# Turning normalised tokens with VectorE's 32x32 transpose and DMAs through DRAM instead of TensorE

## The chip, the cores and the metric

The kernel runs on one core of a Trainium2 chip. TensorE (PE) multiplies, VectorE (DVE) and ScalarE (ACT) work on elements, GpSimd (POOL) does a few odd operations, and SyncE (SP) issues nearly all DMAs. The metric is the device time of one execution in microseconds. Before the change it is 1166.89 us, the median of 3 runs (1166.68 to 1167.87).

## What is computed

The reference is a transformer of two layers on x of shape (4, 512, 256), all in fp32. Each of the four steps normalises its input first and adds its result to x:

```python
x = x + _L0_attn_ref(_layernorm(x, axis=-1), L0_attn_w_project, L0_attn_w_out)
x = x + _L0_ffn_ref(_layernorm(x, axis=-1), L0_ffn_router_w, L0_ffn_router_b, L0_ffn_expert_w, L0_ffn_expert_b)
x = x + _L1_attn_ref(_layernorm(x, axis=-1), L1_attn_w_qkv, L1_attn_w_proj)
x = x + _L1_ffn_ref(_layernorm(x, axis=-1), L1_ffn_gate_W_packed, L1_ffn_gate_scales, L1_ffn_up_W_packed, L1_ffn_up_scales, L1_ffn_down_W_packed, L1_ffn_down_scales)
```

Layer 0's attention is causal, with 16 heads of 16, over 512 tokens. Its second step mixes 8 experts: for each of 256 outputs the two best of 8 router logits weigh the experts' products, so there are two dense products of 256 x 2048 for every token. Layer 1's attention has 16 heads of 128 in 4 groups, and it reads the axis of length 4 as the sequence: each token attends to 4 tokens. Its last step is a gated unit of 2048 inner units (tanh GELU of a gate times an up product, then a down product) whose weights come as 4-bit codes with scales.

## The kernel before

**Layout.** The 2048 tokens lie in `xres` as 16 tiles of 128 tokens with 256 features each. Four tiles form a block (`NBLK` = 4), so a normalised block `xn` is 128 x 4 x 256. The host has put the tokens in such an order that, in each tile, every 32 partitions hold a closed set of layer 1's short sequences.

**Turning.** Products need the features on the partitions: `xT` is 128 x 2 x 512 (two halves of the features, 512 tokens). `transposed` (line 206) turns one half of a block with four TensorE transposes of 128 x 128 against an identity into one PSUM tile of the pool `dn` (two buffers, shared with most products), and ScalarE copies it to SBUF. There are sixteen such conversions: four for layer 0's attention (`inputs_T`, line 571), which the change leaves alone, and the twelve that it touches, whose PSUM tiles are named `xT_ps`: the four blocks of the experts (`hidden_pieces`, line 264), the four of layer 1's attention (`start_pieces` with `into_T`, lines 989 and 981), and the four of the gated unit (`first_pieces`, line 1122, makes the first one, `x_first`; `normed_T`, line 213, the other three). In the experts' blocks the copy of the second half adds 16 to the last feature (`last_16`, line 86), with which the biases are folded into the weights.

**Order.** Until the gated unit, PE, DVE, POOL and ACT run in the order in which the code is written (`manual_schedule`, line 73); SP does so only through the first batches (line 899), and after that the framework's scheduler orders it, where earlier code has precedence. The written order comes from a planner: work beside the attention is cut into pieces by generators, each `yield need(engine, cost, gap, cond)` says what a piece costs (about microseconds), how many slots must have passed since the stream's last piece and on what condition it may go; `fill` (line 149) is one slot and emits ready pieces, stream by stream, until the slot's budgets of PE and DVE are used up. Streams inserted at the front go first. The paces of the experts' pieces follow `made()`, the number of finished steps of the weights.

**Stages.** Layer 0's attention fills the first 385 us or so, with the projections and the experts' pieces between its batches. Block b of the experts starts when block b of the attention is done (line 811). `logit_pieces` and `result_pieces` call `dense` (line 230), whose stationary operand is 128 columns of `xT`. Then layer 1's pools open, `wqkv` is loaded by ten DMAs and `wpj` by one (lines 963 to 973), and `start_pieces(0)` goes first in the slots (line 1148); it issues the turning, then four pieces of values (line 1001). For each of 16 pairs of block and group, `project1`, `score`, `softmax_1`, `softmax_2`, `mix` and `output` follow, with slots between them. `start_pieces(j + 1)` starts while the first group of block j is worked on. When the experts are done, the 4-bit weights are loaded and decoded in further pieces (`weight_in_pieces`, line 1128) and `x_first` is made. In the gated unit (lines 1214 to 1281) all engines are ordered by the framework's scheduler. `inner(j)` makes gate and up products for 16 groups of 128 inner units (`gate_up`, line 946) and the tanh GELU; `down(j)` follows one block later.

Of the kernel before, what the change touches and what calls it, by code (L numbers as in the profile page):

```python
# [8 lines left out]
F32 = mybir.dt.float32  # L9
# [7 lines left out]
P = 128  # L17
# [15 lines left out]
def tile_transformer(  # L33
# [48 lines left out]
    nc.vector.memset(half_t, 0.5)  # L82
    minus_12 = const.tile([P, 1], F32, name="minus_12")
    nc.vector.memset(minus_12, -12.0)

    last_16 = const.tile([P, 1], F32, name="last_16")
    nc.vector.tensor_scalar(last_16, ident[:, P - 1 : P], 16.0, None, ALU.mult)

    mask32 = const.tile([P, 32], F32, name="mask32")
    nc.vector.tensor_reduce(  # L90
# [23 lines left out]
    def need(engine, cost, gap=0, cond=None):  # L114
        return engine, cost, gap, cond
# [83 lines left out]
    def layernorm(j, pool, small, deinterleave=False):  # L199
# [3 lines left out]
        normed.clear()  # L203
        return out[0]

    def transposed(xn, hc, ps_pool, tag, name):

        ps = ps_pool.tile([P, 4, P], F32, tag=tag, name=name)
        for t in range(4):
            nc.tensor.transpose(ps[:, t, :], xn[:, t, hc * P : (hc + 1) * P], ident)  # L210
        return ps

    def normed_T(j, pool, small, ps_pool, tag, deinterleave=False, out_pool=None):
        xn = layernorm(j, pool, small, deinterleave)
        xT = (out_pool or pool).tile([P, 2, 512], F32, tag="xT", name=f"xT{j}")
        for hc in range(2):
            ps = transposed(xn, hc, ps_pool, tag, f"xT_ps{j}_{hc}")
            nc.scalar.copy(xT[:, hc, :], ps.rearrange("p t q -> p (t q)"))
        return xT

    def add_residual(g, ps):
        nc.vector.tensor_tensor(xres[:, g, :], xres[:, g, :], ps, ALU.add)  # L222
# [7 lines left out]
    def dense(ps, g, w, pair):  # L230

        xT = xTs[g // 4]
        for hc in range(2):
            nc.tensor.matmul(  # L234
                ps, lhsT=xT[:, hc, (g % 4) * P : (g % 4 + 1) * P],
                rhs=w[:, hc, 2 * pair : 2 * pair + 2, :].rearrange("p e o -> p (e o)"),
                start=hc == 0, stop=hc == 1,
            )
# [25 lines left out]
    def hidden_pieces(b):  # L264

        out = []
        done = (4 * b - 5, 1)
        last = b == NBLK - 1
        yield from norm_pieces(b, b1, b2, out, cond=lambda: b < 2 or done in halves)
        xT = b2.tile([P, 2, 512], F32, tag="xT", name=f"xT{b}")  # L270
        for hc in range(2):
            yield need("PE", 0.5, 0 if hc else 1 + last)
            ps = transposed(out[0], hc, ps_dn, "dn", f"xT_ps{b}_{hc}")
            ps = ps.rearrange("p t q -> p (t q)")
            if hc:
                nc.scalar.activation(xT[:, hc, :], ps, AF.Identity, bias=last_16)
            else:
                nc.scalar.copy(xT[:, hc, :], ps)
        normed.clear()
        xTs[b] = xT  # L280

    def logit_pieces():
# [663 lines left out]
    def gate_up(ps, w, xT, jj, par):  # L946
        for half in range(2):
            nc.tensor.matmul(  # L948
                ps, lhsT=wgu[:, w, half, jj, par * P : (par + 1) * P], rhs=xT[:, half, :],
                start=half == 0, stop=half == 1,  # L950
            )

# [6 lines left out]
    with ExitStack() as l1:  # L959
# [20 lines left out]

        def into_T(out, to, name):

            for hc in range(2):
                yield need("PE", 0.5, 0 if hc else 2)
                ps = transposed(out[0], hc, ps_dn, "dn", f"{name}_ps{hc}")
                nc.scalar.copy(to[:, hc, :], ps.rearrange("p t q -> p (t q)"))  # L986
            normed.clear()

        def start_pieces(j):

# [34 lines left out]
        def score(p):  # L1025

            qT, kT = state.pop("qk")
            ps = ps_dn.tile([P, 4, HPK, 32], F32, tag="dn", name=f"s1_{p}")
            for t in range(4):
                for c in range(NC):  # L1030
                    at = t * P + 32 * c
                    nc.tensor.matmul(  # L1032
                        ps[32 * c : 32 * c + 32, t], lhsT=kT[:, at : at + 32],
                        rhs=qT[:, :, at : at + 32], start=True, stop=True,
                    )
            state["s"] = ps
# [44 lines left out]
        def mix(p):  # L1081
            j, kv = divmod(p, NKV)
            v, pT = state[j][1], state.pop("p")
            avs = [
                ps_a.tile([P, 4, HPK, 32], F32, tag="a", name=f"a_{p}_{c}") for c in range(NC)
            ]
            for t in range(4):
                for c in range(NC):
# [125 lines left out]
    with ExitStack() as f1:  # L1214
        wd_p = f1.enter_context(tc.tile_pool(name="f1_w", bufs=1))
        d2 = f1.enter_context(tc.tile_pool(name="f1_2", bufs=2))
        d1 = f1.enter_context(tc.tile_pool(name="f1_1", bufs=1))
        d3 = f1.enter_context(tc.tile_pool(name="f1_3", bufs=3))
        ps_gu = f1.enter_context(tc.tile_pool(name="f1_gu", bufs=2, space=PSUM))
        ps_o = f1.enter_context(tc.tile_pool(name="f1_o", bufs=2, space=PSUM))  # L1220

        wd = wd_p.tile([P, NJ, 2, HID], F32, name="wd")

        def inner(j):
            xT = normed_T(j, d2, d2, ps_dn, "dn", deinterleave=True) if j else x_first
            it = d2.tile([P, NJ, 2, 512], F32, tag="it", name=f"it{j}")
            for jj in range(NJ):
                for par in range(2):
                    n = f"{j}_{jj}_{par}"
                    if firsts:  # L1230
                        gp, up = firsts
                        firsts.clear()
                    else:
                        gp = ps_gu.tile([P, 512], F32, tag="g", name=f"g_{n}")
                        up = ps_gu.tile([P, 512], F32, tag="u", name=f"u_{n}")
                        gate_up(gp, 0, xT, jj, par)
                        gate_up(up, 1, xT, jj, par)
# [5 lines left out]
                    nc.vector.tensor_tensor(sq, sq, gp, ALU.mult)  # L1243
                    nc.scalar.activation(th, sq, AF.Tanh, scale=0.7978845608028654)  # L1244
                    nc.vector.scalar_tensor_tensor(th, th, 1.0, gp, ALU.add, ALU.mult)  # L1245
                    nc.vector.scalar_tensor_tensor(
                        it[:, jj, par, :], th, 0.5, up, ALU.mult, ALU.mult
                    )
                if j < 2 and jj % 4 == 3:
                    at = 4 * j + 2 * (jj // 4)  # L1250
                    for _ in dequant_pieces(
                        d2, d1, f"d{at}", [down_w[at + i] for i in range(2)],
                        [
                            lambda b, i=i: down_s[at + i, b : b + 1, :].to_broadcast([16, HID])
                            for i in range(2)
                        ],
                        wd[:, at : at + 2], lambda emit, slots=1: emit(),
                    ):
                        pass
            return it  # L1260

        def down(j, it):
            for t in range(4):
                ps = ps_o.tile([P, HID], F32, tag="o", name=f"y_{j}_{t}")
                for c in range(2 * NJ):
                    nc.tensor.matmul(  # L1266
                        ps, lhsT=it[:, c // 2, c % 2, t * P : (t + 1) * P],
                        rhs=wd[:, c // 2, c % 2, :], start=c == 0, stop=c == 2 * NJ - 1,
                    )
                add_residual(4 * j + t, ps)  # L1270
# [4 lines left out]
        pending = None  # L1275
        for j in range(NBLK):
# [62 lines left out]
```

## Time and profile before

| what | us |
|---|---|
| median of 3 runs | 1166.89 |
| span of the profiled execution | 1164.9 |
| PE busy | 1144.1 |
| DVE busy | 812.4 |
| ACT busy | 481.9 |
| transposes on `xT_ps` (96) and their weight loads, PE busy | 15.6 and 11.5 |

The profiled execution's own time beside its span is not recorded; its span is 2.0 us below the runs' median. In the profile, busy time counts instructions between their start and end, and matmuls overlap in the pipeline, so a busy PE is not PE at its peak: the distance between two starts is the better measure. An idle time in brackets ends with what released the instruction. "issue" stands for waits that the profile does not show. A timeline row merges instructions of one kind; its second column is then the stretch from the first start to the last end.

### The profile page before, as it was taken

Reading aid. Unit: us, or ns where it says so; the run is one execution under the profiler, and the core shown is the slowest. Engines: PE = TensorE matmul, PEld = TensorE weight load, DVE = VectorE, ACT = ScalarE, POOL = GpSimd, SP = SyncE. Lnnn points to the kernel's source line nnn. Section 1 sums busy time; section 2 is a strip of 40 time slices with the busy share of each in tenths; the row PEclk is TensorE's granted clock in tenths of the full one; section 3 lists DMA queues with packets and bytes.
Section 4 is the critical chain, followed back from the end, with each engine's and each line's share of the span. In section 5 each row is a group of like instructions: output and inputs, shape, how many; then the busy total and the mean of one; then the engine's idle time right before and its main releaser. Section 6 shows DMA issues by size and latency. Waiting matters only on the chain.

```text
span 1164.9 us, 18575 instructions
## 1 busy us (share of the span) xinstructions
PE 1144.1 (98%) x7182; PEld 662.6 (57%) x7182; DVE 812.4 (70%) x1788; ACT 481.9 (41%) x1095; POOL 108.2 (9%) x153
## 2 busy tenths in 40 slices
PE   9999999999998999999999999999999999999998
PEld 5666555555554445555555555566544475484487
DVE  6675899999988844868663776687699835716710
ACT  1444555555655542444443444444344313303300
POOL 8322221212112000000000000000000000000000
PEclk9999999999999999999999999999999999999999
DMA  4440100000000500000000001110110000000000
GB/s 130 118 120 2 27 12 1 2 2 2 2 2 1 181 1 1 1 1 0 1 1 1 1 1 46 33 51 19 27 46 1 0 1 19 0 1 19 1 19 18
DMA packets 21527, 26.46 MB, mean 23 GB/s; under 512 B 5160, under 2 KB 15144, under 8 KB 21440
## 3 DMA queue, kind: packets, MB, share of 16 engines
q1 hardware_dynamic: 20624, 24.10, 7.6%
q10 hardware_dynamic: 816, 1.18, 0.4%
q8 instruction: 56, 0.92, 0.3%
q14 instruction: 31, 0.25, 0.1%
HBM read 18.97 MB, written 2.10 MB: 18 GB/s over the span
## 4 chain that ended last, share of the span: by engine, by line
PE 82%; DVE 13%; issue 2%; ACT 1%; POOL 1%; SPq 0%; DMA 0%; POOLq 0%; DVEq 0%; ACTq 0%
PE qk_ps L1019 11%; PE y L1266 9%; PE o L1110 9%; PE g L948 9%; PE u L948 9%; PE lg_ps L234 8%; PE eo L234 7%; PE s L668 3%; PE s L716 3%; DVE mx L687 3%; PE av L752 2%; PE v_ps L1001 2%; PE qk_ps L539 2%; PE a L1090 1%; PE s L1032 1%
## 5 line engine op out<-in xcount | busy, mean ns | idle before, releaser
L1019 PE MATMUL qk_ps<-xT,wqkv 128*128 128x512 f32 x320 | 148.9, 599 | 2.3 <-ACT part L323 1.2
L234 PE MATMUL lg_ps<-rw,xT 128*128 128x512 f32 x256 | 122.5, 601 | 1.4 <-ACT xT L986 0.3
L234 PE MATMUL eo<-ew,xT 128*128 128x512 f32 x256 | 121.5, 600 | 0.8 <-ACT lg L297 0.5
L1110 PE MATMUL o<-wpj,oT 128*128 128x256 f32 x512 | 119.1, 382 | 0.0
L1266 PE MATMUL y<-wd,it 128*128 128x256 f32 x512 | 111.8, 379 | 0.0
L1110 PEld LDWEIGHTS o<-wpj,oT 128*128 128x128 f32 x512 | 95.9, 190 | 27.5 <-issue 14.3
L1266 PEld LDWEIGHTS y<-wd,it 128*128 128x128 f32 x512 | 97.0, 190 | 15.0 <-issue 2.2
L687 DVE TENSOR_REDUCE mx<-s 128x1 f32<-128x384 f32 (+3 forms) x176 | 100.5, 633 | 0.2 <-PE s L681 0.2
L1019 PEld LDWEIGHTS qk_ps<-xT,wqkv 128*128 128x128 f32 x320 | 59.1, 190 | 71.4 <-issue 57.4
L725 ACT ACTIVATE pt<-s 128x512 f32<-128x512 f32 (+1 forms) x176 | 84.1, 565 | 35.9 <-PE s L716 35.9
L948 PE MATMUL g<-xT,wgu 128*128 128x512 f32 x192 | 90.4, 593 | 0.0
L948 PE MATMUL u<-xT,wgu 128*128 128x512 f32 x192 | 90.2, 592 | 0.0
L323 ACT ACTIVATE part<-eo,c 128x256 f32<-128x256 f32 x128 | 53.6, 471 | 84.7 <-PE eo L234 74.8
L735 POOL TENSOR_SCALAR_AFFINE_SELECT pt<-pt 128x256 f32<-128x256 f32 (+2 forms) x88 | 62.4, 716 | 246.9 <-ACT pt L725 246.7
L1244 ACT ACTIVATE th<-sq 128x512 f32<-128x512 f32 x64 | 40.3, 630 | 87.8 <-DVE sq L1243 87.8
L234 PEld LDWEIGHTS lg_ps<-rw,xT 128*128 128x128 f32 x256 | 46.1, 190 | 46.1 <-issue 37.3
L234 PEld LDWEIGHTS eo<-ew,xT 128*128 128x128 f32 x256 | 46.1, 190 | 45.7 <-issue 38.3
L222 DVE TENSOR_TENSOR xres<-xres,y 128x256 f32<-128x256 f32 x16 | 6.7, 421 | 92.5 <-PE y L1266 92.5
L297 ACT COPY lg<-lg_ps 128x512 f32<-128x512 f32 x64 | 37.6, 588 | 73.5 <-PE lg_ps L234 73.5
L185 POOL TENSOR_TENSOR ln_rs<-rs_v,minus_half 128x4 f32<-128x4 f32 x15 | 16.6, 1103 | 552.2 <-DVE rs_v L184 440.0
L1245 DVE SCALAR_TENSOR_TENSOR th<-th,g 128x512 f32<-128x512 f32 x63 | 43.2, 686 | 29.3 <-ACT th L1244 29.2
L948 PEld LDWEIGHTS u<-xT,wgu 128*128 128x128 f32 x192 | 36.5, 190 | 45.9 <-issue 44.7
(240 smaller groups left out, 1782.5 us busy)
## 6 DMA issues: line engine op xcount, KB each, us to landing
qk<-stage SPq DMA_DIRECT2D x56, 64.0 KB, 2.4
wqkv<-in_w_qkv SPq DMA_DIRECT2D x8, 320.0 KB, 6.4
rw<-in_router_w SPq DMA_DIRECT2D x8, 256.0 KB, 4.8
ew<-in_expert_w SPq DMA_DIRECT2D x8, 256.0 KB, 5.5
wpj<-in_w_proj SPq DMA_DIRECT2D x1, 2048.0 KB, 12.5
out<-xres SPq DMA_DIRECT2D x4, 512.0 KB, 2.7
xres<-in_x SPq DMA_DIRECT2D x3, 512.0 KB, 4.8
dq_wgu<-in_gate_w SPq DMA_DIRECT2D x8, 128.0 KB, 2.4
```

The source lines that it names most:

```text
L234: nc.tensor.matmul(ps, lhsT=xT[:, hc, (g % 4) * P : (g % 4 + 1) * P], rhs=w[:, hc, 2 * pair : 2 * pair + 2, :].rearrange("p e o -> p (e o) ...
L297: nc.scalar.copy(lg[:, 2 * pair : 2 * pair + 2, :].rearrange("p e o -> p (e o)"), ps)
L323: nc.scalar.mul(part[:, e % 4], ps[:, i], c[:, e : e + 1])
L687: nc.vector.tensor_reduce(maxes[n % 2][:, h, gs[0] : gs[0] + nb], ps[:, : nb * nk].rearrange("p (b k) -> p b k", b=nb), AX.X, ALU.max,)
L725: nc.scalar.activation(pt[:, i, : nb * nk], tiles[2 * pair + i][:, : nb * nk], AF.Exp, scale=0.25)
L735: nc.gpsimd.affine_select(out=last, in_=last, compare_op=ALU.is_ge, fill=0.0, base=0, pattern=pattern, channel_multiplier=-1,)
L948: nc.tensor.matmul(ps, lhsT=wgu[:, w, half, jj, par * P : (par + 1) * P], rhs=xT[:, half, :], start=half == 0, stop=half == 1,)
L1019: nc.tensor.matmul(ps, lhsT=wqkv[:, hc, kv, h, :], rhs=xT[:, hc, :], start=hc == 0, stop=hc == 1,)
L1110: nc.tensor.matmul(ys[t // 2][:, t % 2], lhsT=state["o"][:, h, t * P : (t + 1) * P], rhs=wpj[:, HPK * kv + h, :], start=kv == 0 and h == 0 ...
L1244: nc.scalar.activation(th, sq, AF.Tanh, scale=0.7978845608028654)
L1245: nc.vector.scalar_tensor_tensor(th, th, 1.0, gp, ALU.add, ALU.mult)
L1266: nc.tensor.matmul(ps, lhsT=it[:, c // 2, c % 2, t * P : (t + 1) * P], rhs=wd[:, c // 2, c % 2, :], start=c == 0, stop=c == 2 * NJ - 1,)
```

## The change

Tokens of the twelve conversions are turned in another way. VectorE transposes each 32 x 32 square of `xn` in one instruction, which leaves each group of 32 partitions with its own tokens but the features of all 8 groups of 32 along the row. Four DMAs, one for each 32 partitions, write these rows to a DRAM tile `by_hidden`, sorted by feature (runs of 512 B), and a fifth reads them back over `xT` with the features on the partitions (runs of 2 KB). All five are issued on SP. The columns of `xT` are then in another order: 32 tokens of tile 0, of tile 1, and so on for each group of 32 partitions. For the experts the transpose writes with a step of four, so that a tile is every fourth column, and `dense` reads every fourth column. Layer 1's attention, where a token needs only its own 32 partitions, takes columns and partitions in the new order; `gate_up` reads the columns in runs of 32 in the old one. The addition of 16 is a VectorE instruction on one column of `xn`. In the plan a conversion is one DVE piece, and the stream may go on three slots later. In the gated unit, norm and turning of the next block are written in the third of the eight steps of `inner`. The 96 transposes and 24 ScalarE copies go.

```diff
-    last_16 = const.tile([P, 1], F32, name="last_16")
-    nc.vector.tensor_scalar(last_16, ident[:, P - 1 : P], 16.0, None, ALU.mult)
...
+    rows_out = ctx.enter_context(
+        tc.tile_pool(name="rows_out", bufs=2, space=bass.MemoryType.DRAM)
+    )
+
+    def turned(xn, xT, name, tiles_inside=False):
+
+        order = "p h (b j t) -> p (h b) t j" if tiles_inside else "p h (b t j) -> p (h b) t j"
+        nc.vector.transpose(
+            xT.rearrange(order, t=4, j=32), xn.rearrange("p t (b j) -> p b t j", j=32)
+        )
+        by_hidden = rows_out.tile([HID, 4, P], F32, tag="by_hidden", name=f"{name}_rows")
+        for a in range(4):
+            nc.sync.dma_start(
+                out=by_hidden.rearrange("(b i) a x -> a i b x", i=32)[a],
+                in_=xT[32 * a : 32 * a + 32].rearrange("p h (b x) -> p (h b) x", x=P),
+            )
+        nc.sync.dma_start(out=xT, in_=by_hidden.rearrange("(h p) a x -> p h (a x)", p=P))
...
-    def normed_T(j, pool, small, ps_pool, tag, deinterleave=False, out_pool=None):
...
     def dense(ps, g, w, pair):
...
-                ps, lhsT=xT[:, hc, (g % 4) * P : (g % 4 + 1) * P],
+                ps, lhsT=xT[:, hc, g % 4 :: 4],
...
     def hidden_pieces(b):
...
-        for hc in range(2):
-            yield need("PE", 0.5, 0 if hc else 1 + last)
-            ps = transposed(out[0], hc, ps_dn, "dn", f"xT_ps{b}_{hc}")
-            ps = ps.rearrange("p t q -> p (t q)")
-            if hc:
-                nc.scalar.activation(xT[:, hc, :], ps, AF.Identity, bias=last_16)
-            else:
-                nc.scalar.copy(xT[:, hc, :], ps)
+        yield need("DVE", 1.5)
+        nc.vector.tensor_scalar(
+            out[0][:, :, HID - 1], out[0][:, :, HID - 1], 16.0, None, ALU.add
+        )
+        turned(out[0], xT, f"xT{b}", tiles_inside=True)
         normed.clear()
+        yield need("PE", 0.0, 3)
         xTs[b] = xT
...
     def gate_up(ps, w, xT, jj, par):
         for half in range(2):
             nc.tensor.matmul(
-                ps, lhsT=wgu[:, w, half, jj, par * P : (par + 1) * P], rhs=xT[:, half, :],
+                ps.rearrange("p (t a j) -> p t a j", a=4, j=32),
+                lhsT=wgu[:, w, half, jj, par * P : (par + 1) * P],
+                rhs=xT[:, half].rearrange("p (a t j) -> p t a j", t=4, j=32),
...
         def into_T(out, to, name):
 
-            for hc in range(2):
-                yield need("PE", 0.5, 0 if hc else 2)
-                ps = transposed(out[0], hc, ps_dn, "dn", f"{name}_ps{hc}")
-                nc.scalar.copy(to[:, hc, :], ps.rearrange("p t q -> p (t q)"))
+            yield need("DVE", 1.4)
+            turned(out[0], to, name)
             normed.clear()
+            yield need("PE", 0.0, 3)
...
         def score(p):
...
-                    at = t * P + 32 * c
+                    at = c * P + 32 * t
                     nc.tensor.matmul(
-                        ps[32 * c : 32 * c + 32, t], lhsT=kT[:, at : at + 32],
+                        ps[32 * t : 32 * t + 32, c], lhsT=kT[:, at : at + 32],
...
         def mix(p):
...
-                    r = slice(32 * c, 32 * c + 32)
+                    r = slice(32 * t, 32 * t + 32)
                     nc.tensor.matmul(
-                        avs[c][:, t], lhsT=v[r, t, kv, :], rhs=pT[r, t], start=True, stop=True
+                        avs[t][:, c], lhsT=v[r, c, kv, :], rhs=pT[r, c], start=True, stop=True
                     )
-            oq = oT.rearrange("p h (t c q) -> p c t h q", c=NC, q=32)
+            oq = oT.rearrange("p h (t c q) -> p t c h q", c=NC, q=32)
...
         def inner(j):
-            xT = normed_T(j, d2, d2, ps_dn, "dn", deinterleave=True) if j else x_first
+            xT = xTs.pop(j)
...
+                if jj == 2 and j + 1 < NBLK:
+                    xTs[j + 1] = d2.tile([P, 2, 512], F32, tag="xT", name=f"xT2_{j + 1}")
+                    turned(
+                        layernorm(j + 1, d2, d2, deinterleave=True), xTs[j + 1], f"xT2_{j + 1}"
+                    )
```

More of the change, by code (lines that the diff above doesn't have):

```diff
@@ L211, in transposed @@
         return ps
-    def normed_T(j, pool, small, ps_pool, tag, deinterleave=False, out_pool=None):
-        xn = layernorm(j, pool, small, deinterleave)
-        xT = (out_pool or pool).tile([P, 2, 512], F32, tag="xT", name=f"xT{j}")
-        for hc in range(2):
-            ps = transposed(xn, hc, ps_pool, tag, f"xT_ps{j}_{hc}")
-            nc.scalar.copy(xT[:, hc, :], ps.rearrange("p t q -> p (t q)"))
-        return xT
     def add_residual(g, ps):
@@ L267, in hidden_pieces @@
         done = (4 * b - 5, 1)
-        last = b == NBLK - 1
         yield from norm_pieces(b, b1, b2, out, cond=lambda: b < 2 or done in halves)
         xT = b2.tile([P, 2, 512], F32, tag="xT", name=f"xT{b}")
-        for hc in range(2):
-            yield need("PE", 0.5, 0 if hc else 1 + last)
-            ps = transposed(out[0], hc, ps_dn, "dn", f"xT_ps{b}_{hc}")
-            ps = ps.rearrange("p t q -> p (t q)")
-            if hc:
-                nc.scalar.activation(xT[:, hc, :], ps, AF.Identity, bias=last_16)
-            else:
-                nc.scalar.copy(xT[:, hc, :], ps)
+        yield need("DVE", 1.5)
[3 more added lines that the diff above has]
+        turned(out[0], xT, f"xT{b}", tiles_inside=True)
         normed.clear()
+        yield need("PE", 0.0, 3)
         xTs[b] = xT
@@ L981, in into_T @@
         def into_T(out, to, name):
-            for hc in range(2):
-                yield need("PE", 0.5, 0 if hc else 2)
-                ps = transposed(out[0], hc, ps_dn, "dn", f"{name}_ps{hc}")
-                nc.scalar.copy(to[:, hc, :], ps.rearrange("p t q -> p (t q)"))
+            yield need("DVE", 1.4)
+            turned(out[0], to, name)
             normed.clear()
+            yield need("PE", 0.0, 3)
         def start_pieces(j):
@@ L1028, in score @@
             ps = ps_dn.tile([P, 4, HPK, 32], F32, tag="dn", name=f"s1_{p}")
-            for t in range(4):
-                for c in range(NC):
-                    at = t * P + 32 * c
+            for c in range(NC):
+                for t in range(4):
+                    at = c * P + 32 * t
                     nc.tensor.matmul(
-                        ps[32 * c : 32 * c + 32, t], lhsT=kT[:, at : at + 32],
+                        ps[32 * t : 32 * t + 32, c], lhsT=kT[:, at : at + 32],
                         rhs=qT[:, :, at : at + 32], start=True, stop=True,
@@ L1086, in mix @@
             ]
-            for t in range(4):
-                for c in range(NC):
-                    r = slice(32 * c, 32 * c + 32)
+            for c in range(NC):
+                for t in range(4):
+                    r = slice(32 * t, 32 * t + 32)
                     nc.tensor.matmul(
-                        avs[c][:, t], lhsT=v[r, t, kv, :], rhs=pT[r, t], start=True, stop=True
+                        avs[t][:, c], lhsT=v[r, c, kv, :], rhs=pT[r, c], start=True, stop=True
                     )
             oT = c2.tile([P, HPK, 512], F32, tag="oT", name=f"oT{p}")
-            oq = oT.rearrange("p h (t c q) -> p c t h q", c=NC, q=32)
+            oq = oT.rearrange("p h (t c q) -> p t c h q", c=NC, q=32)
             state["o"] = oT
@@ L1275, in tile_transformer @@
         pending = None
+        xTs[0] = x_first
         for j in range(NBLK):
```

## The prediction

> **What bounds the kernel now.** I read the page first: busy times, then the chain that ended last.
>
> ```profile
> PE 1144.1 (98%) x7182; PEld 662.6 (57%) x7182; DVE 812.4 (70%) x1788; ACT 481.9 (41%) x1095; POOL 108.2 (9%) x153
> ...
> PE 82%; DVE 13%; issue 2%; ACT 1%; POOL 1%; SPq 0%; DMA 0%; POOLq 0%; DVEq 0%; ACTq 0%
> ```
>
> TensorE is busy nearly throughout and is 82% of the chain; VectorE has 13%, nearly all of it in layer 0's attention. A table of stretches separates the stages: from 160 to 380 us PE is busy 213.5 of 220 and DVE 203.2, so they alternate as the limit; from 400 to 820 us PE has 415.5 of 420 and DVE 282; after 820 us PE has 340 of 345. So TensorE time removed after 400 us is worth its full length, before that about nothing, and a wait that TensorE cannot fill after 380 us is lost in full.
>
> Next I asked for the transposes. Line 210 issues 96 on `xT_ps`, eight in each of twelve places, and the timeline shows what eight displace. Columns are start, duration, engine, line.
>
> ```profile
> 587.30 0.60 PE L210 MATMUL xT_ps<-ident,xn 128*128 128x128 f32 x4
> 587.50 0.59 ACT L1023 COPY qT<-qk_ps 128x512 f32<-128x512 f32 x1 [0.64 <-PE qk_ps L1019]
> ...
> 588.14 0.66 PE L210 MATMUL xT_ps<-ident,xn 128*128 128x128 f32 x4 [0.24 <-ACT qT L1023]
> 588.46 1.09 ACT L986 COPY xT<-xT_ps 128x512 f32<-128x512 f32 x2
> ...
> 589.12 1.98 PE L234 MATMUL lg_ps<-rw,xT 128*128 128x512 f32 x4 [0.32 <-ACT xT L986]
> ```
>
> The next product starts 589.12 - 587.30 = 1.82 us after the first transpose. Half of that is waiting: both `dn` buffers of PSUM are held until ScalarE has copied. Without waits, at 1049 us, eight take 1050.24 - 1049.36 = 0.88 us.
>
> **What goes.** I take start differences, place by place, after 400 us: experts' block 3 at 418 us 1.81; layer 1's blocks 1 to 3, 1.82, 1.82 and 0.89 + 0.84 = 1.73; `x_first` 0.53 + 1.13 = 1.66; gated unit's blocks 2 and 3, 0.88 each. Its block 1 gives 0.90 + 0.11 + 0.11 + 0.43 = 1.55 in a stretch where DVE is busy 20.00 of 20 us (840 to 860), so the new DVE work there is set against it: 1.55 - 1.27 = 0.3. Sum: 10.9 us. With the waits left out it would be about 7 (eight places at 0.88). The 24 copies of about 0.6 us on ScalarE go too; at 41% busy, that is worth nothing beyond the PSUM waits already counted. What is late next after 400 us is again TensorE.
>
> **What comes, on VectorE.** Twelve 128x1024 block transposes.
>
> ```profile
> L1243 DVE TENSOR_TENSOR sq<-sq,g 128x512 f32<-128x512 f32 x63 | 43.1, 685 | 1.4
> ...
> L397 DVE TENSOR_TENSOR lg<-lg,m 128x1024 f32<-128x1024 f32 x32 | 38.9, 1245 | 0.0
> ...
> L1041 DVE STREAM_TRANSPOSE sm<-s 128x512 f32<-128x512 f32 x16 | 11.4, 715 | 28.1 <-PE s L1032 28.1
> ```
>
> A 512-element transpose takes 0.715 us, and 512 more elements add 1.245 - 0.685 = 0.56, so one takes 1.27 us. The experts' four add 16 to a column (128x4, about 0.17 us by line 184). Those four also write with a step of four elements. No row has a stepped write; the nearest is line 90's reduction of 128 elements read with a step, 364 ns against about 286 interpolated between the 64- and 384-element reductions (220 and 548): 0.6 ns an element, 0.6 us for 1024. Bounds 0 to 0.6 each; I take 0.
>
> In layer 0, three places: DVE +1.44 each, TensorE relieved of 2.5, 1.6 and 1.3. At 94 us TensorE's next wait is for a DVE maximum, so block 0 costs 1.4; in the other two both engines are near full and I take zero. Block 0's first logits also come three slots later (some 13 us). Cover: attention goes on meanwhile, and the displaced products (92, 96 and 101 us, 5 us of PE) shift to later slots. If that cover fails they are paid after 400 us. Layer 0 in all: +1.4, bounds -3 to +6. Experts' blocks 1 and 2 have room: ready at 171 and 288 us, their first logits are evicted at 221 and 363.
>
> **What comes, on the queue.** Each conversion issues five DMAs on SP, four writes of 128 KB and one read of 512 KB that waits for all four. In quiet the rows give: an issue every 0.6 us, 2.4 us to landing (`qk<-stage`), 2.7 us for 512 KB (`out<-xres`). So 1.8 + 2.4 + 2.7 = 6.9 us plus 1.3 on DVE, 8 us; up to 10.5 if the read takes the 4.8 us of `xres<-in_x`. Three slots hide that where a slot is 3.5 us (400 to 690 us). SP stands still meanwhile; behind it queue only the 4-bit weights' loads (700 to 760 us), which already wait for buffers between 719.7 and 738.3.
>
> One place is not quiet: **the start of layer 1's attention**, block 0. Chronologically:
>
> ```profile
> 385.86 5.94 SPq L968 DMA_DIRECT2D wqkv<-in_w_qkv  x10
> ...
> 389.10 0.60 PE L210 MATMUL xT_ps<-ident,xn 128*128 128x128 f32 x4
> ...
> 390.69 7.12 PE L1001 MATMUL v_ps<-wqkv,xT 128*128 128x512 f32 x16
> ...
> 392.11 0.41 SPq L973 DMA_DIRECT2D wpj<-in_w_proj  x1
> ```
>
> ```profile
> 392.00:398.00 6.00, 6.00 (x15) 2.66 (x14) 5.82 (x11) 2.72 (x6) 0.00 (x0) 1.00 1.00 366
> 398.00:404.00 6.00, 5.71 (x14) 2.33 (x13) 5.97 (x26) 5.03 (x17) 0.00 (x0) 1.00 0.93 295
> 404.00:410.00 6.00, 6.00 (x15) 2.66 (x14) 3.53 (x14) 2.56 (x7) 0.52 (x1) 1.00 0.00 1
> ```
>
> The last two columns are the DMA engines' busy share and GB/s: they are full until 404 us. `wpj`, 2 MB, would take 5.7 us at 366 GB/s, but lands 12.5 us after its issue: it queued behind `wqkv`. The new writes stand after all eleven loads in the code, need memory that the same release frees, and need a DVE result besides. I take it that they are issued after `wpj` (392.5 us) and move only when it has landed, 404.7. Writes 2 us, read 2.7: `xT` is there at 409.5 us, where values started at 390.7. TensorE runs in the written order, so it stops at the values. The two extra slots pull about three products ahead, 3 x 1.72 = 5.2 us. Loss: 18.8 - 5.2 = 13.6 us; this place's own saved 1.59 us is inside that. Bounds: -1.6 (writes go first) and +16.
>
> After such a stop the clock may be low. The ten matmuls that open the kernel took 6.68 us against 10 x 0.43; that bounds it at 2.4 us, below at 0 (granted clock 1.00 in every stretch). I take 1.2. The Trainium skill ("TensorE: Matmul & The Clock Gate", Part 1) says that a window of 3.4 us without work halves the clock until a busy window has passed, an estimate of 1.7 us here and a sum 0.5 higher; no row here shows it.
>
> **Strided operands.** The experts' 512 weight loads read `xT` with a step of four. Loads take 190 ns and start 429 ns apart, so up to 0.43 is hidden. By line 90's ratio they would take 0.19 + 128 x 0.6 ns = 0.27: free. The skill ("SBUF — State Buffer", Door 1) counts 16-byte lines and charges each access that opens a new one; a step of four fp32 is just that, and without a price its sum runs from mine to the third rival's. The gated unit's moving operand in runs of 32 is as in line 1032, whose matmuls take 273 ns like line 752's: 0.
>
> **Sum.** Profiled span 1164.9: -10.9 + 1.4 + 13.6 + 1.2 = +5.3, so 1170.2. The runs' median stands 2.0 above the span (1166.89), so **1172.2 us**.
>
> **Rivals.**
> - *The writes get ahead of the loads* (scheduled earlier, or not held by the ring). No stop, no cold clock, block 0 saves its 1.6: -10.9 + 1.4 - 1.6 = -11.1, so 1156: faster. For: the writes are small. Against: `wpj`'s landing. If they get in between `wqkv` and `wpj`, `xT` is there at about 403 and the total comes out near 1166, no change.
> - *Another stop besides*: the writes of layer 1's block 3 (after 707 us) stand behind the 4-bit loads until 738 and the values of 740 wait for some 8 us: 1180. Decides if SP holds a load that waits for a buffer ahead of them. Against: those loads become ready later.
> - *Stepped weight loads over 0.43 us*: each 0.1 us beyond costs 512 x 0.1 = 51 us: above 1200. Decides at 2.3 times today's duration; the line 90 ratio is 1.3.
>
> **How the numbers follow.** Forecast 0.55 (own range 1166 to 1179), writes first 0.22, in between 0.07, another stop 0.10, weight loads 0.06. The range 1154 to 1184 leaves out the weight loads and the lower part of "writes first". A measurement can tell 0.2%, 2.3 us. Faster: 0.22 + half of "in between" + the forecast's low edge, 0.28; same 0.14; slower 0.58.
>
> **What would show it.** Right: TensorE idle some 14 us between 395 and 410 us, ended by DMA `xT`; `by_hidden` writes of that block landing after `wpj`; no line 210 on `xT_ps`; block transposes near 1.27 us; `LDWEIGHTS` of line 234 under 0.43. Wrong: values starting before 400 us, or DVE gaining length from the stepped write.

## The result, and the profile after

The changed kernel takes 1184.2 us (median of 4 runs, 1183.4 to 1184.8), the kernel before 1167.1 beside it: ratio 1.0147, 95% interval 1.0133 to 1.0161. That is 17.1 us slower, where 5.3 had been forecast. The span of the profiled execution is 1182.9 us.

First the page of the changed kernel: busy times, the granted clock in 40 slices, and the chain that ended last.

```profile
PE 1146.3 (97%) x7086; PEld 716.8 (61%) x7086; DVE 827.4 (70%) x1803; ACT 468.3 (40%) x1071; POOL 105.4 (9%) x153
...
PEclk9997999999999899999999999999999999999999
...
PE 82%; DVE 10%; SPq 2%; issue 2%; DMA 2%; ACT 1%; POOL 1%; DVEq 0%; POOLq 0%; ACTq 0%
```

96 matmuls are gone and TensorE is not less busy (1144.1 before). Weight loads gained 54 us, DMAs and SP's queue now have 2% of the chain each, and the clock has two dents, near 90 and 400 us. The waits of TensorE (what for: us in total, times, longest) name the places:

```profile
PE v_ps L1006 <- DMA xT<-xT_rows: 12.1, 1, 12.1
PE av L756 <- DVE qk L704: 6.7, 8, 4.0
PE qk_ps L1024 <- ACT qT L1028: 3.9, 1, 3.9
PE g L952 <- DVE th L1250: 1.5, 1, 1.5
```

There are three stops: 4.0 us at 89 us, 12.1 at 401 us, 3.9 at 743 us. All idle times of TensorE over 0.6 us add up to 27.0 us, before to 5.9. Behind each of the three the granted clock is low. In the stretches below (their bounds and length in us, the busy times of the five engines, then granted clock, DMA share, GB/s) it was 1.00 throughout in the kernel before:

```profile
90.00:96.00 6.00, 2.70 (x48) 2.22 (x52) 5.90 (x11) 0.37 (x1) 0.29 (x1) 0.67 0.35 72
96.00:102.00 6.00, 6.00 (x45) 4.37 (x42) 2.36 (x10) 2.06 (x4) 2.81 (x4) 0.50 0.33 103
102.00:108.00 6.00, 6.00 (x34) 3.02 (x36) 3.58 (x8) 1.10 (x2) 0.00 (x0) 0.70 0.01 1
...
412.00:418.00 6.00, 4.82 (x8) 2.27 (x9) 0.00 (x0) 0.58 (x1) 0.00 (x0) 0.65 0.02 7
```

In steps of 2 us, TensorE's busy time multiplied by the missing share of the clock gives 6.2 us lost at 92 to 106, 1.5 at 406 to 418, 1.6 at 746 to 752, and 1.7 at 172 to 178, behind an idle time of only 0.57 us: 11.0 us in all.

Start times show where the delay arises. The last maximum of layer 0 (`mxT`) starts 9.7 us later than before, the first values of layer 1 22.5 later (390.7 and 413.2), the gated unit 20.1 later, and the span is 18.0 longer. So layer 0 costs 9.7 where I had 1.4, the start of layer 1 12.8 more, and layer 1's attention gives back 2.4 only. From the gated unit's start to the end it is 334.8 us before and 332.7 after, the gain forecast there (0.88 + 0.88 + 0.3).

The stop at the start of layer 1, in order of time:

```profile
390.64 5.66 SPq L974 DMA_DIRECT2D wqkv<-in_w_qkv  x10
...
395.76 1.25 DVE L210 STREAM_TRANSPOSE xT<-xn 128x1024 f32<-128x1024 f32 x1
...
396.50 0.38 SPq L979 DMA_DIRECT2D wpj<-in_w_proj  x1
...
397.36 7.07 SPq L215 DMA_DIRECT2D xT_rows<-xT  x4
...
409.20 0.38 SPq L219 DMA_DIRECT2D xT<-xT_rows  x1
...
413.18 7.34 PE L1006 MATMUL v_ps<-wqkv,xT 128*128 128x512 f32 x13 [12.12 <-DMA xT<-xT_rows]
```

This is the forecast's picture: all eleven loads first, the writes behind `wpj`, the read only at 409.2 when the writes had landed. The stop in layer 0 was not in it:

```profile
88.35 0.33 PE L701 MATMUL mxT<-ident,mx 128*128 128x128 f32 x1
...
88.48 2.29 DVE L191 TENSOR_SCALAR xn<-xres,ln_mv,ln_rs 128x256 f32<-128x256 f32 x4 [0.52 <-POOL ln_rs L182]
...
90.80 0.17 DVE L278 TENSOR_SCALAR xn<-xn 128x4 f32<-128x4 f32 x1
91.00 1.99 DVE L210 STREAM_TRANSPOSE xT<-xn 128x1024 f32<-128x1024 f32 x1
...
92.84 0.41 DVE L704 TENSOR_TENSOR qk<-qk,mxT 128x256 f32<-128x256 f32 x1
...
93.30 1.93 PE L756 MATMUL av<-pt,va 128*32 128x128 f32 x32 [3.97 <-DVE qk L704]
```

VectorE works in the written order: normalising, adding 16 and transposing the experts' first block stand ahead of the small subtraction (line 704) for which TensorE's next products wait. The transpose with the stepped write takes 1.99 us instead of the 1.27 reckoned. The same place in the kernel before, where the subtraction comes right behind the normalisation and TensorE has transposes and the first logits to do meanwhile:

```profile
90.95 0.41 DVE L700 TENSOR_TENSOR qk<-qk,mxT 128x256 f32<-128x256 f32 x1
...
92.09 1.98 PE L234 MATMUL lg_ps<-rw,xT 128*128 128x512 f32 x4 [0.24 <-ACT xT L278]
...
94.00 1.08 PE L752 MATMUL av<-pt,va 128*32 128x128 f32 x32
```

So the stop by itself does not make TensorE late: it reaches these products at 93.30, and at 94.00 before. It takes the place of transposes that are gone and of logits that come later. What is lost on the spot is the low clock behind it, 6.2 us here; the logits have to be made up for later.

The third stop is one of written order too. A decode of the 4-bit weights waits on VectorE for its loads, its next step on ScalarE stands ahead of a copy (line 1028), and TensorE waits for that copy:

```profile
743.22 0.43 DVE L931 TENSOR_SCALAR dq_mgu<-dq_wgu 128x512 int32<-128x512 int32 x1 [3.67 <-DMA dq_sgu<-in_up_s]
...
744.15 1.15 ACT L933 ACTIVATE dq_bgu<-dq_mgu,minus 128x1024 f32<-128x1024 int32 x1 [5.40 <-DVE dq_mgu L932]
...
746.79 3.27 PE L1024 MATMUL qk_ps<-xT,wqkv 128*128 128x512 f32 x4 [3.93 <-ACT qT L1028]
```

### The profile page after: what moved, and what is told of

The parts are those of the page before. It is cut to its first block, busy times and chain, and to the rows that moved or that the text cites. A ratio compares the mean times of both kernels' runs of the same rounds, so it can differ in the third digit from the quotient of the medians.

```text
span 1182.9 us, 18572 instructions
## 1 busy us (share of the span) xinstructions
PE 1146.3 (97%) x7086; PEld 716.8 (61%) x7086; DVE 827.4 (70%) x1803; ACT 468.3 (40%) x1071; POOL 105.4 (9%) x153
## 4 chain that ended last, share of the span: by engine, by line
PE 82%; DVE 10%; SPq 2%; issue 2%; DMA 2%; ACT 1%; POOL 1%; DVEq 0%; POOLq 0%; ACTq 0%
PE qk_ps L1024 10%; PE y L1276 9%; PE g L952 9%; PE u L952 9%; PE eo L241 8%; PE lg_ps L241 8%; PE o L1115 8%; PE s L672 3%; PE s L720 3%; DVE mx L691 2%; PE av L756 2%; PE v_ps L1006 2%; PE qk_ps L543 2%; PE a L1095 1%; PE s L1037 1%
## 5 line engine op out<-in xcount | busy, mean ns | idle before, releaser
L241 PE MATMUL eo<-ew,xT 128*128 128x512 f32 x256 | 127.8, 622 | 1.1 <-ACT part L327 0.9
L241 PE MATMUL lg_ps<-rw,xT 128*128 128x512 f32 x256 | 126.4, 619 | 0.0
L241 PEld LDWEIGHTS eo<-ew,xT 128*128 128x128 f32 x256 | 75.7, 312 | 28.7 <-ACT part L327 5.4
L241 PEld LDWEIGHTS lg_ps<-rw,xT 128*128 128x128 f32 x256 | 76.3, 312 | 26.7 <-issue 3.6
L739 POOL TENSOR_SCALAR_AFFINE_SELECT pt<-pt 128x256 f32<-128x256 f32 (+2 forms) x88 | 59.3, 678 | 261.4 <-ACT pt L729 260.9
L1246 ACT ACTIVATE sq<-g 128x512 f32<-128x512 f32 x63 | 37.5, 595 | 103.7 <-PE g L952 103.4
## 6 DMA issues: line engine op xcount, KB each, us to landing
wpj<-in_w_proj SPq DMA_DIRECT2D x1, 2048.0 KB, 11.1
```

Source lines behind the costliest of these rows:

```text
L241: nc.tensor.matmul(ps, lhsT=xT[:, hc, g % 4 :: 4], rhs=w[:, hc, 2 * pair : 2 * pair + 2, :].rearrange("p e o -> p (e o)"), start=hc == 0, ...
L739: nc.gpsimd.affine_select(out=last, in_=last, compare_op=ALU.is_ge, fill=0.0, base=0, pattern=pattern, channel_multiplier=-1,)
```

## The experiments

The kernel before ran on the same chip beside each of them, at 1166.3 to 1167.1 us. Low clock below is what is lost by it, in us, reckoned as above.

**1. The stepped loads**, in the kernel before; the order on every engine stays. ScalarE's eight copies have to write the experts' columns with the step, too.

```diff
-                ps, lhsT=xT[:, hc, (g % 4) * P : (g % 4 + 1) * P],
+                ps, lhsT=xT[:, hc, g % 4 :: 4],
...
+            to = xT[:, hc].rearrange("p (q t) -> p t q", t=4)
```

> The kernel before (1167 us), with one thing of the change alone: ScalarE's eight copies write the experts' columns with a step of four, and the 512 weight loads of the dense products read with that step. Theory A (the loss comes from three stops of TensorE and the low clock after them; a stepped load of some 0.31 us is hidden below a matmul's 0.43): 1167, within 2 us. Theory B (the longer loads themselves make the products of the experts longer: distances between their starts sum to 255.3 us in the changed kernel against 235.8): the time rises by much of 19.5 us, above 1178. A value between, say 1170 to 1174, would mean that only loads right behind a wait, where nothing covers them, are paid.

Measured: 1172.3 us, ratio 1.0040 (1.0026 to 1.0054), so +5.7 us: between the theories, where only some of the loads are paid. Groups of this kernel (busy time, mean ns of one): the experts' loads and, for comparison, those of layer 1's projections.

```profile
L1019 PEld LDWEIGHTS qk_ps<-xT,wqkv 128*128 128x128 f32 x320 | 59.1, 190 | 67.8 <-issue 53.0
...
L234 PEld LDWEIGHTS lg_ps<-rw,xT 128*128 128x128 f32 x256 | 75.8, 313 | 28.0 <-ACT part L323 2.1
L234 PEld LDWEIGHTS eo<-ew,xT 128*128 128x128 f32 x256 | 75.9, 312 | 27.3 <-issue 2.2
```

Which of them are paid follows from the distances between starts. Between two experts' products with another experts' product ahead of them (278 pairs) it stays 0.43 us: the longer load is hidden. Where short score matmuls stand ahead (41 pairs, nearly all in layer 0), it grows from 0.507 to 0.628 us, by the whole 0.12 us that the load gained: 4.9 us. With the other places, after transposes above all, these distances gain 8 us, more than the total does. The copies grew as well, from 0.57 to 0.69 us each to 1.06 to 1.21, and with them TensorE's waits at the first and the fourth block (0.71 instead of 0.24 us, 0.45 instead of 0.01). So up to 0.9 of the 5.7 us can be theirs.

**2. The experts by TensorE** in the changed kernel, in contiguous columns (`hidden_pieces` and `dense` as before).

> The changed kernel (1184 us), with the four blocks of the experts turned by TensorE again, in contiguous columns; the rest stays. Theory A: layer 0 gets back its 9.7 us of delay (the 4 us stop at 89 us and the low clock after it), block 3 pays its eight transposes again (1.8), the stop at the start of layer 1 stays: about 1176. Theory B: besides that the products between 410 and 700 us are as short as before: 1170 or less.

Measured: 1178.3 us. Layer 0 does get its delay back, but the values start only 2.3 us earlier (410.9): they wait for a DMA, and the stop before them grew from 12.1 to 15.0 us. A gain ahead of a wait for something else is eaten by that wait. The total still falls by 5.9 us, 2 less than theory A had: 272 dense matmuls are done before the values, where there were 260.

**3. `wpj` behind the turning's writes.**

```diff
             turned(out[0], to, name)
+            if name == "xT1_0":
+                nc.sync.dma_start(out=wpj, in_=w_proj.rearrange("(e p) h -> p e h", p=P))
```

> The changed kernel with one load moved: wpj (2 MB) is issued after the turning DMAs of layer 1's first block instead of ahead of them. If the turning waits behind the loads, as the prediction had it, the 12.1 us stop at 401 us shrinks by the transfer of wpj, 5.7 us at 366 GB/s, and the lower clock after it by part: 1177 to 1178. If the stop were the turning's own latency (transpose, writes, read, some 8 to 10 us from the transpose), it stays: 1184.

Measured: 1184.1 us, the stop 11.1 us. It looks like the rival's number, but the trace shows why it decides nothing: `wpj` was issued at 399.6, still ahead of the read (404.3), which then waited behind it. Experiments 9 and 10 do it properly.

**4. Layer 1's first block by TensorE** (`into_T` takes the transposes for `xT1_0`, and ScalarE copies into the new order of columns).

> The changed kernel, with layer 1's first block alone turned by TensorE again (into the new order of columns). The prediction's step says that this stop is worth 13.6 us and the clock after it 1.2, and that the eight transposes cost about 1.6 and are inside: 1184 less 13 to 15, so 1169 to 1171. If another wait (wqkv itself, or the first pair's softmax) stands right behind the stop, less than half of it comes back: above 1177.

Measured: 1180.7 us; the values start 15.0 us earlier, at 398.2, and only 3.5 us remain. The values now stand earlier in the written order, and so do the slots that follow. The waits of TensorE between 415 and 480 us in this kernel:

```profile
PE eo L241 <- DVE sm L1056: 2.7, 1, 2.7
PE v_ps L1016 <- DMA xT<-xT_rows: 1.6, 1, 1.6
PE eo L241 <- ACT part L327: 1.5, 1, 1.5
PE eo L241 <- ACT lg L301: 0.7, 1, 0.7
```

The second block's values start at 461.5, where they started at 462.2. Between the two places TensorE waits these 6.5 us, and it does 48 dense matmuls there instead of 44, and 24 output products and 32 score products that come behind the second block's values in the changed kernel. Such an experiment also changes the plan, and is no pure price of the stop.

**5. The first decode later.**

```diff
-        yield need("DVE", 0.9)
+        yield need("DVE", 0.9, 3 * (n == "gu0"))
```

> The changed kernel (1184 us) with one gap in the plan: the first decoding piece of the 4-bit weights may go only three slots after its 18 loads were issued, not in the same slot. Theory A: the 3.9 us stop at 743 us is TensorE waiting for ScalarE behind a decode that waits for its loads, and the low clock after it costs 1.7 (granted 0.95 for 6 us, then 0.77 for 6): both go, 1178 to 1179. Rival: the decode moved back is then missing at the end of layer 1's attention, or another wait stands at the same place: 1183 or more.

Measured: 1183.6 us, the rival. The stop at 743 us has gone, and 3.6 us come back at 749 us, for another reason:

```profile
740.53 3.87 SPq L921 DMA_DIRECT2D dq_sgu<-in_up_s  x8
...
741.66 1.25 DVE L210 STREAM_TRANSPOSE xT<-xn 128x1024 f32<-128x1024 f32 x1
...
744.51 1.88 SPq L215 DMA_DIRECT2D xT_rows<-xT  x4
...
748.51 0.39 SPq L219 DMA_DIRECT2D xT<-xT_rows  x1
...
752.30 3.75 PE L1006 MATMUL v_ps<-wqkv,xT 128*128 128x512 f32 x4 [3.57 <-DMA xT<-xT_rows]
```

The writes, ready at 742.9, wait until SP has issued the scales' loads at about 0.5 us each. That is the forecast's rival of another stop behind the 4-bit loads; in the changed kernel a decode that waits for the same loads comes first.

**6. The experts' transpose a slot later.**

```diff
-        yield need("DVE", 1.5)
+        yield need("DVE", 1.5, 1)
         nc.vector.tensor_scalar(
```

> The changed kernel with one gap in the plan: VectorE's block transposes of the experts go one slot after the normalisation, so that the subtraction for which TensorE waits at 89 us stands ahead of the 2.16 us of the addition and the transpose. Theory A: the 4.0 us stop goes, and with it the stretch at a granted clock of 0.50 to 0.70 up to 108 us, which costs 0.9 + 3 + 1.8 = 5.7 us of TensorE: layer 0's delay of 9.7 shrinks to 3 or 4 (the stepped loads' share of it), so about 1178. Rival: layer 0's delay is the VectorE work and the logits that come later, and the stop only its sign: above 1182.

Measured: 1193.5 us, 9 us worse. The stop shrinks to 1.8 us, the low clock there is gone, and layer 0 ends as early as before (a late maximum starts at 356.3; 357.1 before, 364.9 after the change). But by 340 us only 190 dense matmuls are done (209 before, 192 after), and layer 1 pays for them, with stops again at 437 to 469 (5.9 us) and 750 us (4.0). The end of layer 0 is no measure of what it cost.

**7. Both first users by TensorE**: the experts (contiguous columns) and layer 1's first block; the new way for the other seven blocks.

> The changed kernel with TensorE's turning for the experts' four blocks (contiguous columns) and for layer 1's first block; the new way stays for layer 1's blocks 1 to 3 and for the gated unit. By the prediction's saved terms it gains 1.82 + 1.82 + 1.73 + 1.66 + 1.76 + 0.3 = 9.1 us against the kernel before (1166.5): 1157 to 1158. Rival (what leaves TensorE's order there is taken up by other waits, of the experts' work on VectorE or of the decode): half of it or less, 1162 to 1167.

Measured: 1158.3 us, ratio 0.9936 (0.9923 to 0.9948): 8.3 us faster than the kernel before (1166.6 there). This is the best version found, and the saved terms of the forecast were right where the turning is hidden.

**8. The new way repaired**: experiments 4, 5 and 6 together.

> The changed kernel with all three stops attacked together: layer 1's first block by TensorE, the experts' transposes one slot later, the first decode three slots after its loads. The stepped loads stay. Theory A (the three stops and their clock, and the stepped loads' 5.7 us, are the whole of the error): before 1166.5 + 1.4 + 5.7 - 9.3 (10.9 without the first block's 1.6) = about 1164. Rival (layer 1 is held by the experts' late work whatever stop is removed, as the first block by TensorE alone gave back only 3.5 us of 15): 1174 or more.

Measured: 1171.8 us, between the two. One long stop is left, 5.3 us at 443 us:

```profile
439.63 1.25 DVE L210 STREAM_TRANSPOSE xT<-xn 128x1024 f32<-128x1024 f32 x1
...
441.03 1.84 SPq L215 DMA_DIRECT2D xT_rows<-xT  x4
...
444.75 0.38 SPq L219 DMA_DIRECT2D xT<-xT_rows  x1
...
448.46 2.04 PE L1016 MATMUL v_ps<-wqkv,xT 128*128 128x512 f32 x2 [5.34 <-DMA xT<-xT_rows]
```

The turning takes 8.8 us in a quiet place (8 forecast). Three slots did not hide it, since VectorE had fallen behind (from 428 us to the transpose it never rests for more than 0.2 us): TensorE reached the values 3.5 us after the transpose's start.

**9 and 10. The loads behind the whole turning**: `wpj` after the read (9), or all but the values' two loads after it (10), in program order. The written order of the other engines is that of the changed kernel.

```diff
+        load_wqkv(wqkv_parts[:1])
...
             turned(out[0], to, name)
+            if name == "xT1_0":
+                load_wqkv(wqkv_parts[1:])
+                load_wpj()
```

> The changed kernel (1184 us), with wpj issued after all five turning DMAs of layer 1's first block, the read included (moved only behind the writes, wpj still went ahead of the read, and the stop stayed at 11.1 us). Theory A (the stop at 401 us is a queue behind the loads): the writes still follow wqkv, but the read lands some 2.7 us after its issue instead of 6.9: the stop falls from 12.1 to about 7, values start near 408. What that gives in the end: if the stop is paid one for one, 1178; if layer 1 is held by other waits, as with the first block by TensorE (15 us earlier values, 3.5 us in the total), 1182 to 1184.

> The changed kernel, with only the two loads of the values' weights ahead of the turning DMAs of layer 1's first block; the other eight of wqkv and wpj follow after the read. Theory A: only the turning's own latency is left, 8.8 us from the start of the transpose as a block in a quiet stretch took it (439.6 to 448.5 us with the three stops repaired): xT is there 8.8 us after its transpose, the stop is about 3.5 us and values start near 405. Rival (latency of the turning itself, not the queue, made the stop): it stays at 10 or more. Total 1179 to 1182, since the same stop taken away wholly gave 3.5 us.

Measured: 1180.3 and 1174.3 us. The stop is 8.0 and 4.0 us instead of 12.1. The timeline of the tenth:

```profile
388.60 1.32 SPq L979 DMA_DIRECT2D wqkv<-in_w_qkv  x2
...
393.74 1.24 DVE L210 STREAM_TRANSPOSE xT<-xn 128x1024 f32<-128x1024 f32 x1
...
395.12 1.84 SPq L215 DMA_DIRECT2D xT_rows<-xT  x4
...
398.82 0.38 SPq L219 DMA_DIRECT2D xT<-xT_rows  x1
...
399.24 3.90 SPq L979 DMA_DIRECT2D wqkv<-in_w_qkv  x8
...
403.00 8.80 PE L1020 MATMUL v_ps<-wqkv,xT 128*128 128x512 f32 x16 [3.97 <-DMA xT<-xT_rows]
```

The read follows the writes after 3.7 us instead of 11.8. The values start 10.2 us earlier and the total falls by 9.9. Of the 10.2 us, 8.1 are the stop; the rest is there at the last maximum of layer 0 (370.1, 372.2 in the changed kernel), where this profile has less low clock. In 9 the stop is 4.1 us shorter and the total 3.9 lower. With the same written order the stop is paid about one for one. The total forecast for the tenth (1179 or more) was wrong, because I had taken experiment 4 for the price of the stop.

**11 and 12. Longer and shorter gaps** on top of experiment 8: the values six slots after the turning instead of three (11), and besides that the logits after two (12).

> The version with all three stops repaired (1171.8 us) with one more edit: layer 1's values go six slots after the turning instead of three. Theory A: there the one stop left, 5.3 us at 443 us for DMA xT of layer 1's second block, and 2 us of clock after it, go: 1164 to 1166, still near the kernel before because the stepped loads (5.7) and the products displaced from layer 0 remain. Rival: the values six slots later are then missing before the next block's first projection, and empty slots take the place of the stop: 1171 or more.

> As the version before it (three stops repaired, values six slots after the turning), and the experts' logits two slots after the turning instead of three. In layer 0 a slot takes some 4.3 us and the turning 8.8. Theory A: layer 0 ends with 20 dense matmuls fewer done than in the kernel before (240 against 260 when the values start), 8.6 us that are paid afterwards, because the first logits come 10 us late; one slot less gives back about a third of it: 2 to 4 us below that version. Rival: logits are not what holds the products back (VectorE's work is), or the turning is not done by then: the same time within 1 us, or a stop at about 100 us.

Measured: 1179.8 and 1177.1 us. In 11 the rival holds. The second block's values start at 455.2 instead of 448.5, and TensorE stops 2.6 and 3.0 us around them for other things (445 and 457 us), so the wait is only written out longer. In its profile the low clock near 100 us came back too, 5.1 us of the 8 that it is slower. In 12 the total falls by 2.7 us, as theory A had it, but TensorE stops 4.0 us at 99 us, as the rival had it, because the logits are there before their `xT`; it decides nothing.

**13 and 14. What layer 0 costs.** On top of experiment 10: the experts' first block alone by TensorE, into the stepped columns (13); all four of them, into contiguous columns (14).

```diff
+        if b == 0:
+            for hc in range(2):
...
+                ps = transposed(out[0], hc, ps_dn, "dn", f"xT_ps{b}_{hc}")
+                to = xT[:, hc].rearrange("p (q t) -> p t q", t=4)
```

> The version with the loads after the turning (1174.3 us), and the experts' first block alone turned by TensorE, into the same columns with a step of four (so the stepped loads stay). Theory A (what is left of layer 0's delay comes from the 4.0 us stop at 89 us, its low clock of 4.6 us, and logits that come 10 us late, and the 4.0 us stop at 733 us with 1.7 of clock only follows from experts that end late): values start near 396 instead of 403, the second stop goes too, 1174.3 - 7 - 5.7 = 1161 to 1163. Rival (layer 0 is held by VectorE's transposes of blocks 1 and 2, or by the stepped loads): less than 4 us, 1171 or more; between, if the stop at 733 stays: 1167.

> The version with the loads after the turning (1174.3 us), with all four blocks of the experts turned by TensorE again into contiguous columns. It differs from the version with both first blocks by TensorE (1158.3) only in layer 1's first block, which keeps the new way with its own latency: a stop of 3.9 us and 1.5 us of clock, less the 1.6 us of transposes saved: 1161 to 1163. Rival (the experts by TensorE with the stop in place gave only 6 us, by its written order): 1167 to 1169.

Measured: 1165.3 us (ratio 0.9997, 0.9987 to 1.0006) and 1165.6 (0.9991, 0.9981 to 1.0000). The first block is worth 9.0 us, and with it the stop at 743 us goes too: the experts' last product starts at 702.7, after 723.7 in experiment 10 and 734.1 in the changed kernel (699.0 before). 14 came out 3 us above its expectation: layer 1's first block costs 7.3 us against experiment 7, even with the loads behind it. Its stop is 2.7 us; 3.4 us of low clock stand in its profile at 26 to 34 us, ahead of everything that was changed.

## Why the prediction was wrong in size

The versions make a ladder from the kernel before to the changed one, one part at a time. The steps add up by construction, to the distance from 1166.6 (beside experiment 7) to 1184.2. Executions of one version lie up to 5 us apart, much of it low clock, so that a step as small as -0.3 tells nothing.

| part | forecast | measured | between |
|---|---|---|---|
| layer 1's blocks 1 to 3 and the gated unit, new way | -9.1 | -8.3 | before, 7 |
| layer 1's first block, loads behind it | | +7.3 | 7, 14 |
| layer 1's first block, loads ahead instead | +14.8 with the line above | +9.9 | 10, changed |
| experts' blocks 1 to 3, with stepped loads | -1.8 | -0.3 | 14, 13 |
| experts' block 0 | +1.4 | +9.0 | 13, 10 |
| sum | +5.3 | +17.6 | |

- **The saved terms** were right: 8.3 of 9.1.
- **The stop behind the loads** was right in mechanism: the writes behind `wpj`, three products pulled ahead (20 dense matmuls, four to a product, instead of 8 between layer 0's last output product and the values), a stop of 12.1 us against some 14. The clock's own term, 1.2, measured 1.5 there. In the ladder the block costs 17.2 us against 13.6 + 1.2 = 14.8. Some 3.4 of that need not be its own: most runs of experiment 14 have a mean granted clock of 0.997, those of 7 around the median 1.000, and no run shows that this comes from the block.
- **The step that failed most** is "block 0 costs 1.4". I priced 1.44 us of VectorE work and asked what TensorE waits for next, but not what stands behind that work on VectorE: the subtraction, for which TensorE stopped 4.0 us. What that stop brought was the low clock (3.2 to 6.2 us in the six profiles with a stop of 4.0 us there), which I had allowed only after the long stop. And "Cover: attention goes on meanwhile" hid less than said: the first logits start at 102.1 instead of 92.1, 192 dense matmuls instead of 209 are done by 340 us, the experts end at 734 instead of 699, and the 4-bit weights' loads move into a place where their decode stops ScalarE and through it TensorE (743 us). So block 0 cost 9.0 us: experiment 13 removes all of it at once. About half is low clock, of which the profile of 10 has 7.8 us and that of 13 3.2; how much each link is worth by itself was not separated.
- **"Strided operands: free"** was wrong. The load became longer than estimated (0.31 us, 0.27 forecast) yet stays below 0.43; but the rule "up to 0.43 is hidden" holds only behind a matmul of 0.43. Behind layer 0's short matmuls the distance grows by the whole 0.12 us, 4.9 us of the 5.7 in experiment 1. The rival's condition, above 0.43, asked for the wrong number. In the ladder this hides in a sum of -0.3: if it costs 4.9 there too, which no run shows, blocks 1 to 3 themselves gave back some 5 where I had 1.8. The Trainium skill ("SBUF — State Buffer", Door 1) charges each access that crosses to a new 16-byte line, and lets one stride for free as far as 4 fp32, which can be read both ways for a step of exactly four; the measured 312 against 190 ns speaks for the penalty.
- **The stepped write** of the transpose was out of bounds: 1.99 to 2.10 us in the changed kernel, 1.24 without the step, so 0.8 more, not 0 to 0.6.

```profile
L210 DVE STREAM_TRANSPOSE xT<-xn 128x1024 f32<-128x1024 f32 x11 | 16.9, 1536 | 0.4 <-PE eo L241 0.2
...
L210 DVE STREAM_TRANSPOSE x_first<-xn 128x1024 f32<-128x1024 f32 x1 | 1.2, 1236 | 0.0
```

Four of the eleven write with the step: (16.9 - 7 x 1.24) / 4 = 2.05 us.

## What to carry to other kernels

A transposition taken off the busiest engine pays where its longer way (here 8.8 us) is hidden, and not at the first use after a stage's start, where nothing covers it and the stage's loads fill the queue: keep the old way there. Putting the loads behind gave back 9.9 of the 17.2 us. When work is put on an engine with a written order, ask what stands behind it there, and who waits for that. A longer weight load is hidden by the matmul ahead of it, not by its own, so look at what is ahead of each one.

## What the hardware showed that was not expected

- The clock after a stop does not follow its length. After 4.0 us at 89 us it was near 0.50 for some 12 us although TensorE counted as busy (6.2 us lost); after the 12.1 us stop it was back within 6 us of the first product (1.5 lost). With the same stop of 1.8 us at 89 us it stayed at 1.00 in experiment 8 and cost 5.1 us in experiment 11. Stretches of 6 us with about 1.7 us lost also come without a stop: at 172 us in the changed kernel behind 0.57 us of idle time, at 26 us in experiments 2, 3 and 7 with none over 0.4 us since 18 us.
- The Trainium skill ("TensorE: Matmul & The Clock Gate", Part 1) lets the full clock return after one busy window of 3.4 us; that gives an estimate of 1.7 us, near the 1.5 and 1.6 us behind the stops at 401 and 743 us, and not what layer 0 showed.
- A step of four fp32 is dear on three engines: a weight load takes 312 ns instead of 190, VectorE's transpose of 1024 elements writes with it in 2.05 us instead of 1.24, and ScalarE's copies of 512 elements in 1.06 to 1.21 us instead of 0.57 to 0.69.
